# A two-stage attention kernel: the first stage's loop regrouped into slots of two query tiles

## The chip, the cores and the metric

The kernel runs on one core of a Trainium2 chip. The metric is the device time of one execution in microseconds, given as the median of several runs. The profile is one such execution, recorded by the hardware profiler, with all its instructions on the five engines: TensorE (PE, with its weight loads as PEld), VectorE (DVE), ScalarE (ACT), GpSimd (POOL) and the queue SP, which issues DMAs.

## What is computed

The input is x, four sequences of 512 tokens with 128 features, in float32. A causal attention with 16 heads of 64 comes first (stage one), then a network of six layers with local attention and a gated feed-forward part (stage two). Each stage works on a layer-normalised input and is added to what went in. The change touches stage one alone:

```python
q = (x @ Wq).reshape(b, s, HEADS, HEAD_DIM)
k = (x @ Wk).reshape(b, s, HEADS, HEAD_DIM)
v = (x @ Wv).reshape(b, s, HEADS, HEAD_DIM)
scores = SCALE * jnp.einsum('bqhd,bkhd->bhqk', q, k)
causal = jnp.triu(jnp.ones((s, s), dtype=x.dtype), k=1)
scores = scores + MASK_PENALTY * causal
attn = jax.nn.softmax(scores, axis=-1)
out = jnp.einsum('bhqk,bkhd->bqhd', attn, v).reshape(b, s, HEADS * HEAD_DIM)
return out @ Wr
```

The mask is a finite penalty of -50 on keys that lie ahead of the query, so all 512 keys are scored for each query.

## The kernel before

**Tiling.** Stage one goes over 4 sequences b, 8 chunks c of two heads each (128 of the 1024 inner features), and 4 tiles t of 128 queries: 128 `Rows` objects, one for each (b, c, t). All matmuls read float32, but for the penalty, which is bfloat16.

**What one tile does.** `scores` (L210) lays the causal penalty into a tile `ps_sc` of two PSUM banks, one for each head, with a matmul of the identity by `pen` (L216, 512 - 128 t columns per head), and adds q times k in four matmuls (L227; each float32 matmul shows as two passes in the trace, and the two heads lie side by side in the array, 64 rows each). VectorE takes the negative row maximum of both heads (L236). `exponents` (L242) is ScalarE's exponential from PSUM to `pr`, once for each head, with the sum of the row as a second result. `normalise` has the reciprocal of the sums on VectorE (L251) and the product of `pr` with it on GpSimd (L252). `transposes` (L263) brings `pr` to `pT` through two banks `ps_pt`, head 0 copied out by ScalarE (L267), head 1 by VectorE (L269).

**What one chunk does.** `make_q` and `make_k` project the next chunk's q and k (L180, L186); ScalarE scales q out of PSUM (L182), VectorE copies k (L188). `make_v` (L195, copy L202) projects 512 columns of V for one tile of keys; it is called once in nearly each chunk. `times_v1` (L280) multiplies V with `pT` for all 512 queries of a chunk, in two halves of two key tiles, into `ps_o`; it uses the array as two times 64 columns. VectorE copies the result behind the second half (L290). After the eight chunks of a sequence `project_out1` (L295) does the output projection.

**Buffers.** `ps_sc`: 2 tiles (four banks). `ps_pt`: 2 banks. `ps_o`: 1 bank. `ps_pj`: 1 bank, shared by the q, k, V and output projections and by the three steps of each layer normalisation (mean L93, variance L102, scale L110), of which a chunk has at most one. `pr` has 3 buffers, `pT` 2.

**Order.** Each engine works through its instructions in the order in which the program calls them; semaphores order the engines against each other. The loop at L311 takes one tile m per step. A step calls the scores and the maximum of tile m, the exponents and the normalisation of tile m-1, the projection of q (t = 0) or k (t = 1), the transposes of tile m-2, a projection of V (t = 0), half a product with V of the chunk before (t = 2 and 3), and a normalisation step (t = 1).

Of the kernel before, what the change touches and what calls it, by code (L numbers as in the profile page):

```python
# [15 lines left out]
P = 128  # L16
# [4 lines left out]
NC = INNER // P  # L21
# [10 lines left out]
def body(ctx: ExitStack, tc: tile.TileContext, a, out: bass.AP):  # L32
# [5 lines left out]
    nc = tc.nc  # L38
    x = a["x"]
    B, S, _ = x.shape  # L40
    L = a["wqkv"].shape[0]
    NT = S // P
# [9 lines left out]
    mm = nc.tensor.matmul  # L52
# [12 lines left out]
    ident16 = const.tile([P, P], BF16, tag="ident16", name="ident16")  # L65
# [66 lines left out]
    with tc.tile_pool(name="s1", bufs=1) as s1, tc.tile_pool(  # L132
# [6 lines left out]
        pen = s1.tile([P, S], BF16, tag="pen", name="pen")  # L139
# [38 lines left out]
        def make_q(b, c):  # L178
            p = bank1()
            mm(p, lhsT=wq[:, c * P : (c + 1) * P], rhs=xnT[b], start=True, stop=True)  # L180
            q = qs[b, c] = s1.tile([P, S], F32, tag="q1", name="q1", bufs=2)
            nc.scalar.activation(q, p, AF.Copy, scale=0.125)  # L182

        def make_k(b, c):
            p = bank1()
            mm(p, lhsT=wk[:, c * P : (c + 1) * P], rhs=xnT[b], start=True, stop=True)  # L186
            k = ks[b, c] = s1.tile([P, S], F32, tag="k1", name="k1", bufs=2)
            nc.vector.tensor_copy(k, p)  # L188

        def make_v(b, j, t):  # L190

            if t == 0:
                vs[b, j] = s1.tile([P, NT, 512], F32, tag="v1", name="v1", bufs=3)
            p = bank1()
            mm(  # L195
                p,
                lhsT=xnT[b][:, t * P : (t + 1) * P],
                rhs=wv[:, j * 512 : (j + 1) * 512],
                start=True,
                stop=True,  # L200
            )
            nc.vector.tensor_copy(vs[b, j][:, t, :], p)  # L202

        class Rows:
# [5 lines left out]
            def scores(self):  # L210
                b, c, t = self.b, self.c, self.t
                sc = self.sc = ps1.tile([P, 2, S], F32, tag="sc", name="ps_sc", bufs=2)
                for h in range(2):


                    mm(  # L216
                        sc[:, h, t * P : S],
                        lhsT=ident16,
                        rhs=pen[:, 0 : S - t * P],
                        start=True,  # L220
                        stop=False,
                        skip_group_check=True,
                    )
                for k0 in range(0, S, S // 2):
                    for h in range(2):
                        rows = slice(h * HD, (h + 1) * HD)
                        mm(  # L227
                            sc[:, h, k0 : k0 + S // 2],
                            lhsT=qs[b, c][rows, t * P : (t + 1) * P],
                            rhs=ks[b, c][rows, k0 : k0 + S // 2],  # L230
                            start=False,
                            stop=True,
                            skip_group_check=True,
                        )
                self.nm = small.tile([P, 2], F32, tag="nm", name="nm")
                nc.vector.tensor_reduce(self.nm, sc, AX.X, ALU.max, negate=True)  # L236

            def exponents(self):
                self.pr = s1.tile([P, 2, S], F32, tag="pr1", name="pr1", bufs=3)
                self.den = small.tile([P, 2], F32, tag="den", name="den")  # L240
                for h in range(2):
# [5 lines left out]
                        accum_out=self.den[:, h : h + 1],  # L247
                    )

            def normalise(self):  # L250
                nc.vector.reciprocal(self.den, self.den)  # L251
                nc.gpsimd.tensor_tensor(  # L252
                    self.pr, self.pr, self.den.unsqueeze(2).to_broadcast([P, 2, S]), ALU.mult
                )
# [53 lines left out]
        make_q(0, 0)  # L308
        make_k(0, 0)

        for m in range(len(rows) + NT + 1):  # L311
            b, c, t = m // (NC * NT), m // NT % NC, m % NT
            more = b < B
            if more:
                rows[m].scores()
            if 0 < m <= len(rows):
                rows[m - 1].exponents()
                rows[m - 1].normalise()

            bn, cn = (b, c + 1) if c + 1 < NC else (b + 1, 0)  # L320
            if bn < B and t == 0:
                make_q(bn, cn)
            if bn < B and t == 1:
                make_k(bn, cn)
            if 1 < m < len(rows) + 2:
                rows[m - 2].transposes()
            if m < NT:
                make_v(0, 0, m)
            if t == 0 and more:
                if c < NT:  # L330
                    make_v(b, 1, c)
                elif b + 1 < B:
                    make_v(b + 1, 0, c - NT)

            bp, cp = (b, c - 1) if c > 0 else (b - 1, NC - 1)
            if 0 <= bp < B and t >= 2:
                times_v1(bp, cp, t - 2)
            if t == 1 and 1 <= c <= 3 and b + 1 < B:
                if c == 1:
                    norms[b + 1] = norm_x(b + 1)  # L340
                norms[b + 1][c - 1]()
            if b > 0 and c == 1 and t == 0:
                project_out1(b - 1)
                norms1[b - 1] = norm_x1(bank1, b - 1)
            if b in range(1, B) and t == 1 and 4 <= c <= 6:
                norms1[b - 1][c - 4]()


# [519 lines left out]
```

## Time and profile before

| | us |
|---|---|
| median of 3 runs (2391.53 to 2397.76) | 2394.96 |
| profiled execution: its time | 2393.57 |
| profiled execution: its span | 2391.8 |
| stage one, from the first scores to the start of the last L295 | 27.0 to 599.4 |

The mean granted TensorE clock over the span is 0.994. Stage one in stretches, busy time of each engine (the view of windows):

| stretch, us | PE | DVE | ACT | POOL | granted clock |
|---|---|---|---|---|---|
| 100 to 200 | 97.2 | 56.4 | 47.4 | 42.4 | 1.00 |
| 200 to 300 | 97.2 | 63.6 | 48.2 | 43.6 | 1.00 |
| 300 to 400 | 96.9 | 57.3 | 45.8 | 40.2 | 1.00 |
| 400 to 500 | 96.7 | 57.0 | 45.6 | 41.6 | 1.00 |
| 580 to 600 | 16.8 | 8.4 | 8.0 | 9.0 | 1.00 |

A timeline line has the start in us from the start of the span, the duration, the engine, the line, the operation, what it writes and reads, the sizes and how many instructions were merged (x8); brackets give idle time of the engine before it and what ended it. A waits line has who waited for whom, the total in us, how often, and the longest. Ends of matmuls are modelled by the profiler, so the distance from the start of one group to the start of the next is the safer measure of what a group takes.

### The profile page before, as it was taken

Reading aid. Unit: us, or ns where it says so; the run is one execution under the profiler, and the core shown is the slowest. Engines: PE = TensorE matmul, PEld = TensorE weight load, DVE = VectorE, ACT = ScalarE, POOL = GpSimd, SP = SyncE. Lnnn points to the kernel's source line nnn. Section 1 sums busy time; section 2 is a strip of 40 time slices with the busy share of each in tenths; the row PEclk is TensorE's granted clock in tenths of the full one; section 3 lists DMA queues with packets and bytes.
Section 4 is the critical chain, followed back from the end, with each engine's and each line's share of the span. In section 5 each row is a group of like instructions: output and inputs, shape, how many; then the busy total and the mean of one; then the engine's idle time right before and its main releaser. Section 6 shows DMA issues by size and latency. Waiting matters only on the chain.

```text
span 2391.8 us, 81676 instructions
## 1 busy us (share of the span) xinstructions
PE 2252.0 (94%) x35057; PEld 1437.8 (60%) x35088; DVE 1695.7 (71%) x2692; ACT 1305.0 (55%) x2166; POOL 1435.4 (60%) x1897
## 2 busy tenths in 40 slices
PE   7999999999799999999999999999999999999997
PEld 3555555555366666666666666666666666666664
DVE  4655656555677777777877778777877777777774
ACT  3454444444254665655565555566555666555662
POOL 2443444444576677766766766766766767766760
PEclk9999999999999999999999999999999999999998
DMA  3000000000222232222322223223232223322220
GB/s 109 1 1 1 1 1 1 1 1 1 55 64 64 54 92 71 57 70 62 83 70 64 66 61 87 68 57 74 63 91 61 70 57 85 78 55 72 61 58 15
DMA packets 91026, 125.82 MB, mean 53 GB/s; under 512 B 25262, under 2 KB 39468, under 8 KB 90668
## 3 DMA queue, kind: packets, MB, share of 16 engines
q1 hardware_dynamic: 90236, 119.02, 20.3%
q8 instruction: 280, 4.59, 0.9%
q10 hardware_dynamic: 432, 1.57, 0.2%
q14 instruction: 78, 0.64, 0.1%
HBM read 20.41 MB, written 1.05 MB: 9 GB/s over the span
## 4 chain that ended last, share of the span: by engine, by line
PE 79%; DVE 13%; issue 4%; ACT 2%; POOL 2%; DMA 1%; SPq 0%; ACTq 0%; POOLq 0%; DVEq 0%
PE ps_proj L414 19%; PE ps_one L510 10%; PE ps_one L605 7%; PE ps_att L580 6%; PE ps_att L548 6%; PE ps_sc L227 5%; PE ps_o L280 5%; PE ps_pt L263 4%; PE ps_proj L638 3%; PE ps_proj L639 3%; PE ps_proj L652 2%; DVE on L590 2%; POOL pr L252 2%; DVE yt L79 1%; PE ps_pj L180 1%
## 5 line engine op out<-in xcount | busy, mean ns | idle before, releaser
L414 PE MATMUL ps_proj<-wqkv,xs 128*128 128x512 f32 x1152 | 568.3, 616 | 31.1 <-ACT vt L492 22.9
L450 POOL TENSOR_TENSOR rot<-rot,t 128x1024 f32<-128x1024 f32 x192 | 453.0, 2360 | 199.7 <-DVE t L439 197.8
L252 POOL TENSOR_TENSOR pr<-pr,den 128x1024 f32<-128x1024 f32 x128 | 242.2, 1893 | 350.3 <-PE ps_pt L263 188.3
L425 ACT ACTIVATE sq<-ps_proj 128x1024 f32<-128x1024 f32 x192 | 196.7, 1025 | 408.4 <-PE ps_proj L414 358.2
L458 POOL TENSOR_TENSOR rot<-rot,ss 128x1024 f32<-128x1024 f32 x192 | 365.2, 1902 | 15.0
L414 PEld LDWEIGHTS ps_proj<-wqkv,xs 128*128 128x128 f32 x1152 | 198.7, 190 | 218.9 <-issue 155.6
L430 DVE TENSOR_REDUCE ss<-sq 128x16 f32<-128x1024 f32 x192 | 233.2, 1214 | 51.1 <-ACT sq L425 50.4
L236 DVE TENSOR_REDUCE nm<-ps_sc 128x2 f32<-128x1024 f32 x128 | 156.7, 1225 | 129.7 <-PE ps_sc L227 129.7
L435 DVE TENSOR_TENSOR rot<-ps_proj,lt 128x1024 f32<-128x1024 f32 x192 | 233.7, 1217 | 0.0
L439 DVE TENSOR_TENSOR t<-ps_proj,lt 128x1024 f32<-128x1024 f32 x192 | 233.2, 1215 | 0.0
L82 POOL TENSOR_TENSOR yt<-y 128x32 f32<-128x32 f32 x288 | 68.7, 239 | 242.9 <-DVE y L80 227.9
L605 PEld LDWEIGHTS ps_one<-aT,wo 128*128 128x128 f32 x1536 | 186.4, 192 | 45.1 <-issue 44.4
L510 PE MATMUL ps_one<-ident,rot 128*128 128x128 f32 x1536 | 211.0, 280 | 1.2 <-ACT qT L513 0.9
L558 DVE TENSOR_REDUCE mx<-ps_att 128x16 f32<-128x1024 f32 x96 | 117.5, 1224 | 126.2 <-PE ps_att L548 125.0
L605 PE MATMUL ps_one<-aT,wo 128*128 128x128 f32 x1536 | 187.3, 275 | 0.4 <-ACT aT L513 0.4
L242 ACT ACTIVATE pr<-ps_sc,nm 128x512 f32<-128x512 f32 x256 | 174.2, 690 | 20.2 <-DVE den L251 15.6
L589 DVE RECIPROCAL rden<-ps_att 128x8 f32<-128x8 f32 x192 | 39.6, 206 | 195.5 <-PE ps_att L580 186.2
L510 PEld LDWEIGHTS ps_one<-ident,rot 128*128 128x128 f32 x1536 | 165.2, 141 | 20.1 <-issue 1.4
L267 ACT COPY pT<-ps_pt 128x512 f32<-128x512 f32 x128 | 74.7, 584 | 181.8 <-PE ps_pt L263 181.8
L580 PEld LDWEIGHTS ps_att<-vw,pT 64*32 64x32 f32 x9216 | 105.1, 105 | 107.7 <-issue 74.0
L580 PE MATMUL ps_att<-vw,pT 64*32 64x65 f32 x9216 | 129.7, 225 | 36.2 <-DVE on L590 27.7
L263 PEld LDWEIGHTS ps_pt<-ident,pr 128*128 128x128 f32 x1024 | 114.4, 141 | 67.4 <-issue 44.6
(127 smaller groups left out, 4061.3 us busy)
## 6 DMA issues: line engine op xcount, KB each, us to landing
vw<-vt SPq DMA_DIRECT2D x1152, 65.0 KB
vw_first<-vt SPq DMA_DIRECT2D x336, 65.0 KB
wqkv<-in_wqkv_dram SPq DMA_DIRECT2D x18, 512.0 KB
wo<-in_wo_dram SPq DMA_DIRECT2D x6, 512.0 KB
w<-in_w_dram SPq DMA_DIRECT2D x6, 341.0 KB
xr<-in_x_dram SPq DMA_DIRECT2D x4, 256.0 KB
out_dram<-tmp_t SPq DMA_DIRECT2D x4, 256.0 KB
w<-in_w_dram SPq DMA_DIRECT2D x12, 64.0 KB
```

The source lines that it names most:

```text
L252: nc.gpsimd.tensor_tensor(self.pr, self.pr, self.den.unsqueeze(2).to_broadcast([P, 2, S]), ALU.mult)
L263: nc.tensor.transpose(pt[:, k * P : (k + 1) * P], self.pr[:, h, k * P : (k + 1) * P], ident)
L414: mm(p[:, c, :], lhsT=u.xs[:, u.T * P : (u.T + 1) * P], rhs=wpart[j][:, c * 512 : (c + 1) * 512], start=True, stop=True,)
L425: nc.scalar.activation(u.sq, u.p[j], AF.Square)
L430: nc.vector.tensor_reduce(u.ss[:, j * HEADS : (j + 1) * HEADS], heads(u.sq), AX.X, ALU.add)
L435: nc.vector.tensor_tensor(heads(t0), heads(pf), lt[:, u.T, 2 * j].unsqueeze(1).to_broadcast([P, HEADS, HD]), ALU.mult)
L439: nc.vector.tensor_tensor(t1.rearrange("p (h t d) -> p h t d", t=2, d=half), pf.rearrange("p (h t d) -> p h t d", t=2, d=half)[:, :, ::-1, :],
L450: nc.gpsimd.tensor_tensor(u.r[j], u.r[j], u.t1, ALU.add)
L458: nc.gpsimd.tensor_tensor(heads(u.r[j]), heads(u.r[j]), u.ss[:, j * HEADS : (j + 1) * HEADS].unsqueeze(2).to_broadcast([P, HEADS, HD]), AL ...
L510: nc.tensor.transpose(tp[:, c * P : (c + 1) * P], src[:, (4 * g + c) * P : (4 * g + c + 1) * P], ident)
L580: mm(o[j * W : (j + 1) * W, h, c * (HD + 1) : (c + 1) * (HD + 1)], lhsT=u.pT[h * HD : (h + 1) * HD, 4 * g + c, j * W : (j + 1) * W], rhs=u ...
L605: mm(y[:, 0:P], lhsT=wo_w[0][:, c, :], rhs=u.aT[:, c, :], start=(c == 0), stop=(c == NC - 1))
```

## The change

The loop takes two tiles per step, a slot. Slot m has the tiles 2m and 2m+1 ("now") and works off those of slot m-1 ("old"). A chunk is two slots: the even one projects q, the odd one k. On TensorE a slot is half a product with V of an earlier chunk, the scores of both tiles, the penalties of both tiles, the transposes of the first old tile, the projection of q or k, the transposes of the second old tile, and then a projection of V (odd slots) or a normalisation step (even slots).

The first half of a chunk's product with V stands at the head of the odd slot behind the one whose last act is the transposes of the chunk's last tile. The penalty is added behind the scores rather than laid down ahead of them. The maximum, the reciprocal and the product with it become calls of their own (`maximum`, `inverse`, `normalise`); the reciprocals stand behind the second transposes of the slot, the second one also behind V's projection. Buffers, sizes and the number of matmuls stay as they were.

```diff
             def scores(self):
                 b, c, t = self.b, self.c, self.t
                 sc = self.sc = ps1.tile([P, 2, S], F32, tag="sc", name="ps_sc", bufs=2)
-                for h in range(2):
-
-
-                    mm(
-                        sc[:, h, t * P : S],
-                        lhsT=ident16,
-                        rhs=pen[:, 0 : S - t * P],
-                        start=True,
-                        stop=False,
-                        skip_group_check=True,
-                    )
                 for k0 in range(0, S, S // 2):
                     for h in range(2):
                         rows = slice(h * HD, (h + 1) * HD)
...
-                            start=False,
-                            stop=True,
+                            start=(k0 == 0),
+                            stop=False,
                             skip_group_check=True,
                         )
+
+            def penalty(self):
+
+                sc, t = self.sc, self.t
+                for h in range(2):
+                    mm(
+                        sc[:, h, t * P : S],
+                        lhsT=ident16,
+                        rhs=pen[:, 0 : S - t * P],
+                        start=False,
+                        stop=True,
+                        skip_group_check=True,
+                    )
+
+            def maximum(self):
+                sc = self.sc
                 self.nm = small.tile([P, 2], F32, tag="nm", name="nm")
                 nc.vector.tensor_reduce(self.nm, sc, AX.X, ALU.max, negate=True)
...
+            def inverse(self):
+                nc.vector.reciprocal(self.den, self.den)
+
             def normalise(self):
-                nc.vector.reciprocal(self.den, self.den)
                 nc.gpsimd.tensor_tensor(
...
-        for m in range(len(rows) + NT + 1):
-            b, c, t = m // (NC * NT), m // NT % NC, m % NT
-            more = b < B
-            if more:
-                rows[m].scores()
-            if 0 < m <= len(rows):
-                rows[m - 1].exponents()
-                rows[m - 1].normalise()
+        last = len(rows) // 2
+        for m in range(last + 5):
+            b, c, odd = m // (2 * NC), m // 2 % NC, m % 2
+            now = rows[2 * m : 2 * m + 2]
+            old = rows[2 * m - 2 : 2 * m] if m else []
+
+            g = (m - 3) // 2
+            if 0 <= g < B * NC:
+                times_v1(g // NC, g % NC, 1 - odd)
+            for r in now:
+                r.scores()
+            for r in now:
+                r.penalty()
+            if now:
+                now[0].maximum()
+            if old:
+                old[0].transposes()
+            if now:
+                now[0].exponents()
+                now[1].maximum()
 
             bn, cn = (b, c + 1) if c + 1 < NC else (b + 1, 0)
-            if bn < B and t == 0:
-                make_q(bn, cn)
-            if bn < B and t == 1:
-                make_k(bn, cn)
-            if 1 < m < len(rows) + 2:
-                rows[m - 2].transposes()
-            if m < NT:
-                make_v(0, 0, m)
-            if t == 0 and more:
-                if c < NT:
-                    make_v(b, 1, c)
-                elif b + 1 < B:
-                    make_v(b + 1, 0, c - NT)
-
-            bp, cp = (b, c - 1) if c > 0 else (b - 1, NC - 1)
-            if 0 <= bp < B and t >= 2:
-                times_v1(bp, cp, t - 2)
-            if t == 1 and 1 <= c <= 3 and b + 1 < B:
+            if bn < B:
+                (make_k if odd else make_q)(bn, cn)
+            if old:
+                old[1].transposes()
+            if now:
+                now[1].exponents()
+                now[0].inverse()
+                now[0].normalise()
+            if m < 2:
+                make_v(0, 0, 2 * m)
+                make_v(0, 0, 2 * m + 1)
+            if odd and c < NT and b < B:
+                make_v(b, 1, c)
+            elif odd and c >= NT and b + 1 < B:
+                make_v(b + 1, 0, c - NT)
+            if now:
+                now[1].inverse()
+                now[1].normalise()
+            if not odd and 1 <= c <= 3 and b + 1 < B:
                 if c == 1:
                     norms[b + 1] = norm_x(b + 1)
                 norms[b + 1][c - 1]()
-            if b > 0 and c == 1 and t == 0:
+            if b > 0 and c == 1 and odd:
                 project_out1(b - 1)
                 norms1[b - 1] = norm_x1(bank1, b - 1)
-            if b in range(1, B) and t == 1 and 4 <= c <= 6:
+            if b in range(1, B) and not odd and 4 <= c <= 6:
                 norms1[b - 1][c - 4]()
```

## The prediction

> **What bounds the kernel now.** I read the page first, then the waits of stage one (40 to 600 us), then its timeline. Stage one ends with the last output projection, L295, which starts at 599.40 us; nothing behind it changes.
>
> ```profile
> PE 2252.0 (94%) x35057; PEld 1437.8 (60%) x35088; DVE 1695.7 (71%) x2692; ACT 1305.0 (55%) x2166; POOL 1435.4 (60%) x1897
> ```
>
> TensorE is busy 94% of the span. What it waits for in stage one, with total, times and longest:
>
> ```profile
> PE ps_pt L263 <- POOL pr L252: 11.2, 22, 1.3
> PE ps_pj L295 <- DVE v L202: 2.4, 3, 0.8
> PE ps_o L280 <- ACT pT L267: 0.2, 1, 0.2
> ```
>
> So only 13.8 us are waits; the rest is groups of matmuls one behind the other. In the timeline the distance from one start to the next is what a group costs:
>
> ```profile
> 212.62 0.38 PE L216 MATMUL ps_sc<-pen,ident 128*128 128x256 bf16 x2
> 212.93 1.14 PE L227 MATMUL ps_sc<-k,q 64*128 64x256 f32 x8
> 213.99 1.09 PE L263 MATMUL ps_pt<-ident,pr 128*128 128x128 f32 x8
> 215.01 1.94 PE L280 MATMUL ps_o<-pT,v 128*64 128x512 f32 x8
> 216.88 0.28 PE L216 MATMUL ps_sc<-pen,ident 128*128 128x128 bf16 x2
> 217.10 1.13 PE L227 MATMUL ps_sc<-k,q 64*128 64x256 f32 x8
> 219.08 1.09 PE L263 MATMUL ps_pt<-ident,pr 128*128 128x128 f32 x8 [0.85 <-POOL pr L252]
> ```
>
> Scores take 1.07, the product with V 1.87, the penalty 0.21 to 0.53 by its columns, transposes 0.87 (1.02 ahead of the product), a projection 0.94 to 0.96. A chunk of four tiles without a normalisation step is 4.36 + 3.32 + 4.27 + 4.17 = 16.12 us.
>
> Why a group costs more than its columns shows in the single rows of 217.10 to 217.85: the first pair of scores (two heads side by side) holds the array 0.32 us, each later pair 0.215, and 0.093 pass between the end of a group's columns and the next group of another array shape (64 rows, 64 columns, or full). That 0.093 is the same at scores to projection, transposes to product, product to penalty and penalty to scores.
>
> **What the change saves on TensorE.** A chunk changes shape 12 times today (each of four scores in and out, each of two products in and out) and 6 times after (product, both scores, penalties: three per slot). Six changes at 0.093 are 0.56 us; longer first pairs fall from four to two (2 x 0.105), and other groups no longer start behind a change (about 0.1). I take 0.86 a chunk, 27 us over 31 chunks, and the POOL waits of 11.2 go too, since a row's transposes now come a slot later. The step from product to scores, from 64 columns to 64 rows, is in no row; its bounds are 0 and two changes (0.19), and I take one, as all four that are seen are equal. Two scores behind each other have the same shape: 0.215 per pair, with a new first pair (+0.105, 6.5 us over 62 slots) as the upper bound and no lower one, since nothing streams faster in these rows. Penalties behind the scores add as many columns as ahead of them.
>
> **What it adds: two waits per chunk.** I walk a slot from the start of its product, with start-to-start distances from the rows. The built order of instructions shows what each waits for. In both slots scores start at 1.87 and the penalties at 1.87 + 0.32 + 7 x 0.215 + 0.093 = 3.80. The first maximum now needs both tiles' scores and its own two penalties ahead of it; a VectorE consumer starts 0.207 behind the end of a matmul's columns (0.42 behind the start of a last score of 0.213).
>
> ```profile
> 224.74 0.60 ACT L182 ACTIVATE q<-ps_pj 128x512 f32<-128x512 f32 x1 [3.03 <-PE ps_pj L180]
> 225.23 0.58 ACT L267 COPY pT<-ps_pt 128x512 f32<-128x512 f32 x1
> ...
> 34.46 1.23 DVE L236 TENSOR_REDUCE nm<-ps_sc 128x2 f32<-128x1024 f32 x1 [0.71 <-PE ps_sc L227]
> 35.60 0.15 DVE L251 RECIPROCAL den<-den 128x2 f32<-128x2 f32 x1
> 35.67 0.67 DVE L188 COPY k<-ps_pj 128x512 f32<-128x512 f32 x1
> ...
> 36.40 1.13 PE L195 MATMUL ps_pj<-wv,xnT 128*128 128x512 f32 x2 [0.93 <-DVE k L188]
> ```
>
> The columns are start, duration, engine, line and operation, and in brackets the idle time before it. They give the steps from start to start: ACT's q to its copy 0.49; 1.14 from a maximum to the next on VectorE; k's copy 0.67 long, then 0.05 until TensorE starts. The last line shows the very wait that I expect in every odd slot: V's projection wants the only ps_pj bank, which k's copy still reads.
>
> Even slot: the first tile's penalties end at 3.80 + 2 x 0.213; maximum at 4.43, done 5.66; exponents 5.75 (0.09 behind it in most rows) and 2 x 0.66 long; q's scaling at 7.07, pT's copy of the second transposes at 7.57, done 8.15. The product of the next slot reads that copy: it starts at 8.20. TensorE alone would be there at 7.41 (3.80 + 0.75 + 0.87 + 0.96 + 1.02), so 0.79 is wait. Before, two or more groups of the next tile lay between a transpose and its product.
>
> Odd slot: penalties are narrower, maximum at 4.22; VectorE then has, in its queue's order, pT copy 5.36 (1.14 behind a maximum), maximum 5.97 (0.61 behind a copy, the step behind L590 of the same 512 columns in stage two), k copy 7.11, done 7.78; V's projection at 7.83 instead of 6.85. It takes 0.96 and 0.093: the slot is 8.89, 0.98 of it wait. Today V's projection follows q, whose ACT scaling lies under the transposes.
>
> Behind the waiting V projection stand the next product and everything after it on TensorE; behind the k copy wait pT's second copy and the reciprocals, which end early enough: the reciprocals, moved behind the pT, k and V copies on VectorE, start POOL's 1.89 at 8.65 and 10.54, done 10.5 and 12.4; the transposes that read them come at 13.4 and 15.3, so the move costs nothing, and would cost what the 2.9 us of cover were short. The exponents that hold the two score banks end by 9.5 of a slot, the scores that want the second come at 11.1. No DMA is moved. The 18 even slots with a normalisation step also need ps_pj, held by q until 7.72, against 0.22 waited today: 8.78, 8.73 and 8.31 (steps of 0.96, 0.91, 0.49).
>
> **The sum.** Slots 2 to 63. Even: 6 x 8.78 + 6 x 8.73 + 6 x 8.31 + 12 x 8.20 + 7.71 (the last, without q) = 261.0. Odd: 27 x 8.89, three without V at 6.99, the last 6.5, and 3 x 7.9 for L295: 291.2. Slot 2 has no product (-1.87). The first two slots, with V's projections waiting in turn for VectorE as at 29.99 to 37.36 today, put slot 2 at 46.6 (today's tile 4: 43.97). The tail waits for POOL's last two rows: transposes at 9.98 and 11.9 of slot 63, two halves of the product, L295 at 17.3, which is 10.8 behind the slot's end. L295 starts at 46.6 + 550.3 + 10.8 = 607.7, 8.3 later. Against the profiled execution (2393.57, span 2391.8) that is 2401.9; against the median 2394.96 it is 2403.
>
> **A rule against it.** Each slot now has an idle stretch of 0.8 to 1 us. In 580 to 600 us today TensorE idles 1.05, 0.57 and 1.26 us, and the windows view gives a granted clock of 1.00 for that stretch as for all of stage one; I count no loss of clock. The Trainium skill, "TensorE: Matmul & The Clock Gate", section "A second HAM failure mode: psum-queue depth-cycling", says that short idle stretches between groups can make the clock fall to half and back. An estimate from its window of 3.4 us: one such window a chunk would cost 1.7 us, 53 in all, and give 2456. The row decides here.
>
> **Rivals.** (a) Faster: the two waits don't bite, because copies land earlier than my walk says. Without them 13 x 0.79 + 18 x 0.47 + 27 x 0.98 = 45 us go: 2358. For it: ACT is busy 55%. Against: both chains run through queues in fixed order. Chance 0.10. (b) No change: each wait about 0.15 shorter (58 x 0.15 = 9): 2394. The bounds of product-to-scores (62 x 0.09 = 5.8 either way) alone nearly reach it. 0.16. (c) Clearly slower: VectorE doesn't start the next operation 0.09 before the one ahead of it has ended, as behind its maxima today, but 0.03 behind, as where one small operation feeds the next (L83 behind L82). That is 0.12 at three places of the odd slot and one of the even, 27 x 0.36 + 31 x 0.12 = 13 more: 2416. It decides once the odd slot passes 9.2. Against it: in stage two VectorE starts 0.09 early behind L430 and L439 too. 0.14. The built order shows the moves as the diff says them, so that the change does nothing is no case.
>
> **Numbers.** My forecast, both waits in full, has 0.60; its own range, from product-to-scores either way, is 2397 to 2409. About 0.3% (7.2 us) can be told from no change, and the forecast is 8.3: of its 0.60 I put 0.20 within. Faster 0.10; same 0.16 + 0.20 = 0.36; slower 0.40 + 0.14 = 0.54. The range takes in (b) and the lower part of (c): 2389 to 2418.
>
> **What would show it.** In stage one after: L263's waits for POOL gone; TensorE waiting some 0.8 us at the product for ACT's pT copy and 1.0 at V's projection for k's copy; product to scores 1.87; slots near 8.2 and 8.9; L295 near 608. Wrong if these waits are below half, if product to scores is far from 1.87, or if the clock falls.

## The result, and the profile after

The changed kernel takes 2416.9 us (median of 5 runs, 2408.12 to 2419.03) where the kernel before takes 2396.45 (5 runs on the same chip): a ratio of 1.008, 95% interval 1.0055 to 1.0106. The forecast was 8.3 us more; the medians are 20.4 apart, the two profiled spans 23.0 (2414.8 and 2391.8).

The last output projection (L302 after, L295 before) starts at 623.46 us, where it started at 599.40 and the forecast had 607.7. Stage one is 24.1 longer and the rest of the span 1.1 shorter, so all of it lies in stage one. After the change the tile's lines are: scores L216, penalty L229, maximum L241, exponents L247, reciprocal L256, GpSimd's product L259, transposes L270 with copies L274 (ScalarE) and L276 (VectorE), product with V L287, its copy aT L297. First the engines' line of the page after:

```profile
PE 2230.5 (92%) x35056; PEld 1446.4 (60%) x35088; DVE 1697.1 (70%) x2692; ACT 1300.6 (54%) x2166; POOL 1435.9 (59%) x1897
```

TensorE has 21.5 us less work on its record and the span is 23.0 longer: 44.5 us more idle. The view of waits, stage one after (40 to 600 us; who waited for whom, total, times, longest), names it:

```profile
PE ps_pj L195 <- DVE k L188: 26.4, 28, 1.1
PE ps_o L287 <- ACT pT L274: 10.7, 12, 0.9
PE ps_pt L270 <- DVE pT L276: 6.2, 6, 1.0
...
PE ps_pj L110 <- ACT q L182: 2.5, 6, 0.4
```

The first two lines are the forecast's two waits, 0.9 each. The third, six times 1.0, was not forecast. The timeline of TensorE after, an odd slot from one product to the next, and the head of the even slot behind it:

```profile
126.45 1.94 PE L287 MATMUL ps_o<-pT,v 128*64 128x512 f32 x8 [0.89 <-ACT pT L274]
128.32 2.00 PE L216 MATMUL ps_sc<-k,q 64*128 64x256 f32 x16
130.25 0.50 PE L229 MATMUL ps_sc<-pen,ident 128*128 128x256 bf16 x4
130.59 1.05 PE L270 MATMUL ps_pt<-ident,pr 128*128 128x128 f32 x8
131.47 1.02 PE L186 MATMUL ps_pj<-xnT,wk 128*128 128x512 f32 x2
132.33 1.04 PE L270 MATMUL ps_pt<-ident,pr 128*128 128x128 f32 x8
134.28 1.13 PE L195 MATMUL ps_pj<-wv,xnT 128*128 128x512 f32 x2 [0.91 <-DVE k L188]
135.34 1.94 PE L287 MATMUL ps_o<-pT,v 128*64 128x512 f32 x8
137.21 2.00 PE L216 MATMUL ps_sc<-k,q 64*128 64x256 f32 x16
```

Product to scores is 128.32 - 126.45 = 1.87, the value taken. The odd slot is 135.34 - 126.45 = 8.89; its wait of 0.89 at the head is the one that the forecast counts at the end of the even slot. From scores to scores, even slots without a normalisation step take 8.22 throughout; those with a mean, variance or scale step take 8.80, 8.73 and 8.33. The walk had 8.20, 8.78, 8.73 and 8.31. So the normal slots are right to 0.02 us, and a chunk takes 17.11 where it took 16.12.

What the walk did not have starts in the slots with a variance step. The timeline after, VectorE, GpSimd and TensorE together, from such a slot (20) into the odd one behind it (21):

```profile
220.59 3.74 POOL L259 TENSOR_TENSOR pr<-pr,den 128x1024 f32<-128x1024 f32 x2 [12.75 <-DVE den L256]
222.16 0.35 DVE L79 TENSOR_SCALAR yt<-rs 128x4 int32<-128x4 int32 x1
222.54 1.82 DVE L80 TENSOR_SCALAR y<-yt 128x4 int32<-128x4 int32 x1
...
226.66 1.22 DVE L241 TENSOR_REDUCE nm<-ps_sc 128x2 f32<-128x1024 f32 x1
...
228.53 0.66 PE L270 MATMUL ps_pt<-ident,pr 128*128 128x128 f32 x4 [1.04 <-DVE pT L276]
230.26 1.19 PE L195 MATMUL ps_pj<-wv,xnT 128*128 128x512 f32 x2 [1.07 <-DVE k L188]
231.38 3.52 PE L287 MATMUL ps_o<-pT,v 128*64 128x512 f32 x8
```

And the same two small operations in the kernel before:

```profile
211.23 1.89 POOL L252 TENSOR_TENSOR pr<-pr,den 128x1024 f32<-128x1024 f32 x1 [2.37 <-PE ps_pt L263]
...
212.99 0.17 DVE L79 TENSOR_SCALAR yt<-rs 128x4 int32<-128x4 int32 x1
213.19 0.17 DVE L80 TENSOR_SCALAR y<-yt 128x4 int32<-128x4 int32 x1
```

L80, on four columns, takes 0.17 before and 1.82 after (1816 to 1820 ns in all six slots). After, GpSimd's two products run one behind the other from 220.59 to 224.33; the middle of that is 222.46. L79 ends at 222.51 and L80 at 224.36, each just behind the end of one product. Before, the product ended at 213.12, and the small operations ran behind it at 0.17. So VectorE stood while GpSimd worked. The late start of the maximum (226.66) makes the transposes wait 1.04, and V's projection 1.07 where 0.91 is usual: odd slots behind a variance step take 10.30, not 8.89.

The last line shows a second loss: the product of slot 21 takes 3.52 where its like took 1.94. The windows view after has it too (the stretch, its length, then busy time and instructions of TensorE, its weight loads, VectorE, ScalarE and GpSimd, then TensorE's granted clock, and two columns on DMA):

```profile
224.00:228.00 4.00, 3.49 (x28) 2.33 (x24) 3.59 (x15) 0.61 (x2) 0.33 (x1) 1.00 0.00 0
228.00:232.00 4.00, 2.40 (x8) 1.01 (x10) 3.39 (x6) 3.25 (x9) 0.96 (x1) 0.90 0.02 4
232.00:236.00 4.00, 4.00 (x18) 1.54 (x16) 0.94 (x3) 0.00 (x0) 2.79 (x2) 0.67 0.00 0
...
616.00:620.00 4.00, 3.24 (x12) 2.10 (x13) 1.38 (x2) 0.81 (x2) 0.74 (x1) 0.61 0.00 0
```

Stage one after has two such stretches, this one and one at 286 us. Both stand directly behind the waits of 1.04 and 1.07 in an odd slot that follows a variance step; slots 21 and 27 take 11.95 and 11.91. The other odd slots behind a variance step have such a wait too and no such stretch. The last window is a third stretch, in the tail of stage one.

### The profile page after: what moved, and what is told of

The parts are those of the page before. It is cut to its first block, busy times and chain, and to the rows that moved or that the text cites. A ratio compares the mean times of both kernels' runs of the same rounds, so it can differ in the third digit from the quotient of the medians.

```text
span 2414.8 us, 81635 instructions
## 1 busy us (share of the span) xinstructions
PE 2230.5 (92%) x35056; PEld 1446.4 (60%) x35088; DVE 1697.1 (70%) x2692; ACT 1300.6 (54%) x2166; POOL 1435.9 (59%) x1897
## 4 chain that ended last, share of the span: by engine, by line
PE 58%; DVE 11%; issue 3%; ACT 2%; POOL 0%; ACTq 0%; POOLq 0%
PE ps_proj L436 19%; PE ps_one L532 10%; PE ps_one L627 7%; PE ps_att L602 6%; PE ps_att L570 5%; PE ps_proj L660 2%; PE ps_proj L661 2%; PE ps_proj L674 2%; DVE on L612 2%; DVE yt L79 1%; DVE rot L457 1%; DVE t L461 1%; ACT vt L514 1%; PE ps_att L559 1%; PE ps_one L93 1%
## 5 line engine op out<-in xcount | busy, mean ns | idle before, releaser
L259 POOL TENSOR_TENSOR pr<-pr,den 128x1024 f32<-128x1024 f32 x128 | 239.9, 1894 | 375.5 <-DVE den L256 375.5
L241 DVE TENSOR_REDUCE nm<-ps_sc 128x2 f32<-128x1024 f32 x128 | 156.0, 1219 | 124.4 <-PE ps_sc L229 124.4
L274 ACT COPY pT<-ps_pt 128x512 f32<-128x512 f32 x128 | 75.1, 587 | 300.6 <-PE ps_pt L270 300.6
L627 PEld LDWEIGHTS ps_one<-aT,wo 128*128 128x128 f32 x1536 | 186.3, 192 | 45.3 <-issue 44.5
L247 ACT ACTIVATE pr<-ps_sc,nm 128x512 f32<-128x512 f32 x256 | 175.2, 696 | 23.1 <-DVE nm L241 23.0
L532 PEld LDWEIGHTS ps_one<-ident,rot 128*128 128x128 f32 x1536 | 165.8, 142 | 20.4 <-issue 2.8
L514 ACT COPY vt<-ps_proj 128x512 f32<-128x512 f32 x192 | 103.1, 589 | 85.6 <-PE ps_proj L436 84.6
```

Source lines behind the costliest of these rows:

```text
L247: nc.scalar.activation(self.pr[:, h, :], self.sc[:, h, :], AF.Exp, bias=self.nm[:, h : h + 1], accum_out=self.den[:, h : h + 1],)
L259: nc.gpsimd.tensor_tensor(self.pr, self.pr, self.den.unsqueeze(2).to_broadcast([P, 2, S]), ALU.mult)
L532: nc.tensor.transpose(tp[:, c * P : (c + 1) * P], src[:, (4 * g + c) * P : (4 * g + c + 1) * P], ident)
L627: mm(y[:, 0:P], lhsT=wo_w[0][:, c, :], rhs=u.aT[:, c, :], start=(c == 0), stop=(c == NC - 1))
```

## The experiments

All edits are made to the changed kernel, unless said otherwise. The runs came in three groups, each on one chip and with its own runs of the kernel before (medians 2393.08, 2392.91 and 2393.36), so the ratios are what to compare. The table gives the usual slot lengths of each profile, from scores to scores, and the granted clock from 60 to 600 us. "Even" and "odd" are slots without a normalisation step in or ahead of them; e8_penalty_ahead is measured from product to product.

| run | median, us | ratio to before (95%) | even | odd | odd behind variance | clock |
|---|---|---|---|---|---|---|
| after | 2416.9 | 1.008 (1.0055–1.0106) | 8.22 | 8.89 | 10.30–11.95 | 0.99 |
| e1_newton_pool | 2404.17 | 1.0042 (1.0026–1.0059) | 8.22 | 8.89 | 8.89 | 1.00 |
| e1b_norm_on_vector | 2409.91 (one run) | – | 8.22 | 8.89 | 9.75 | 0.99 |
| e2_k_copy_first | 2382.54 | 0.996 (0.9945–0.9976) | 8.22 | 7.88 | 9.17 | 1.00 |
| e3_exp_behind_copy | 2426.02 | 1.0124 (1.0108–1.014) | 8.11 | 8.89 | 13.6–14.7 | 0.97 |
| e5_product_behind | 2447.91 | 1.0232 (1.0216–1.0248) | 8.19 | 10.34 | 10.2–10.6 | 0.99 |
| e6_maxima_first | 2478.51 | 1.0358 (1.0344–1.0371) | 9.47 | 8.03 | 10.1–10.3 | 0.95 |
| e7_all | 2473.95 | 1.0345 (1.0316–1.0375) | 9.47 | 8.03 | 9.5–10.9 | 0.94 |
| e8_penalty_ahead | 2432.42 | 1.0175 (1.0158–1.0193) | 8.60 | 9.20 | 10.4 | 1.00 |
| e9_copy_behind | 2402.45 | 1.0039 (1.0025–1.0054) | 7.42 | 8.03 | 10.95–12.67 | 0.98 |
| e10_copy_behind_all | 2370.54 | 0.9911 (0.9892–0.993) | 7.42 | 8.03 | 8.03 | 1.00 |
| e11_k_copy_and_newton | 2374.58 | 0.9931 (0.9913–0.9949) | 8.22 | 7.88 | 7.88 | 1.00 |

**The variance's small operations on GpSimd.** A queue of their own takes them out from under the products:

```diff
-        nc.vector.tensor_scalar(ti, v.bitcast(I32), 1, None, ALU.logical_shift_right)
-        nc.vector.tensor_scalar(y.bitcast(I32), ti, -1.0, 1597463007.0, ALU.mult, ALU.add)
+        if pool_seed:
+            nc.gpsimd.tensor_scalar(y.bitcast(I32), v.bitcast(I32), -0.5, 1597463007.0, ALU.mult, ALU.add)
+        else:
+            nc.vector.tensor_scalar(ti, v.bitcast(I32), 1, None, ALU.logical_shift_right)
+            nc.vector.tensor_scalar(y.bitcast(I32), ti, -1.0, 1597463007.0, ALU.mult, ALU.add)
...
-            rsqrt(rs, NT, nc.vector)
+            rsqrt(rs, NT, eng, pool_seed=eng is nc.gpsimd)
```

`eng` is GpSimd for the six variance steps inside the loop, and VectorE otherwise.

> The changed kernel, with the 13 small operations of stage one's six variance steps on GpSimd behind its two products, not on VectorE beside them (the starting value in one operation). In the changed kernel's trace L80 takes 1.82 us there instead of 0.17, ends with GpSimd's second product, and the odd slot behind is 10.3 us instead of 8.89; two half-clock stretches in stage one follow such slots. Theory (the two engines exclude each other): the odd slots behind a variance step fall to 8.9, no half-clock stretch is left inside stage one, the time falls by 8 to 12 us against the changed kernel. Rival (those slots are long for another reason, such as the PSUM bank held by q): they stay near 10.3 and the time stays within 3 us.

The timeline of GpSimd in this run; its lines stand three further down (L262 is L259):

```profile
223.69 3.74 POOL L262 TENSOR_TENSOR pr<-pr,den 128x1024 f32<-128x1024 f32 x2 [14.45 <-DVE den L259]
227.51 0.19 POOL L80 TENSOR_SCALAR y<-rs 128x4 int32<-128x4 int32 x1
227.79 0.20 POOL L85 TENSOR_TENSOR yt<-y 128x4 f32<-128x4 f32 x1
```

They now follow the products in GpSimd's own queue, 0.28 us each, and nothing on VectorE waits. The odd slots behind a variance step are 8.89 like all others. By the ratios the kernel is 0.4% faster than after, some 9 us, which the theory asked for. A miss: stretches at half clock did not vanish. The profile has one at the start and one at about 207 us, where the slot with the output projection took 18.50 instead of 16.81; e1b_norm_on_vector, the next run, has two more such slots. Behind a variance step neither run has one.

**The same place from the other side: GpSimd's products of these slots on VectorE.** This gives VectorE 2 x 1.23 us more work in the slots in question, and takes away what excludes it.

```diff
+            eng = nc.vector if var_step else nc.gpsimd
...
-                now[0].normalise()
+                now[0].normalise(eng)
...
-                now[1].normalise()
+                now[1].normalise(eng)
```

> The changed kernel, with the two products of exponents and reciprocals of each variance slot on VectorE instead of GpSimd, so that VectorE has some 2.4 us more to do there and GpSimd nothing. If the engines exclude each other, L80 is 0.17 us again and the odd slot behind is shorter than 10.3, about 9.6 (VectorE then reaches the next maximum some 0.7 us late), in spite of the added work. If VectorE is simply overloaded there, the slot becomes longer, about 12.

VectorE's timeline in this run:

```profile
221.74 1.23 DVE L259 TENSOR_TENSOR pr<-pr,den 128x1024 f32<-128x1024 f32 x1
222.89 0.15 DVE L104 TENSOR_SCALAR rs<-ps_pj 128x4 f32<-128x4 f32 x1
223.08 0.17 DVE L79 TENSOR_SCALAR yt<-rs 128x4 int32<-128x4 int32 x1
223.28 0.17 DVE L80 TENSOR_SCALAR y<-yt 128x4 int32<-128x4 int32 x1
```

L80 is back at 0.17 and the slot at 9.75, shorter than 10.30 although VectorE has more to do. A VectorE that is merely overloaded would have made the slot longer. The exclusion is shown from both sides. The Trainium skill, "SBUF — State Buffer", section "Who interferes with whom", says that VectorE and GpSimd share a pair of ports, that `tensor_scalar` can take it in its fast mode, and that whoever comes second is blocked for the whole instruction; L80's 1.82 us beside a GpSimd product of 1.89 agrees. No run here shows which port it was.

**k's copy ahead of the second maximum** in odd slots, so that V's projection gets its bank earlier:

```diff
-                now[1].maximum()
+                if not odd:
+                    now[1].maximum()
...
                 (make_k if odd else make_q)(bn, cn)
+            if now and odd:
+                now[1].maximum()
```

> The changed kernel, with k's copy ahead of the second tile's maximum on VectorE in odd slots; TensorE's order is untouched. Theory (V's projection waits only for that copy): the copy starts at about 6.15 of the slot and ends at 6.83, the wait of 0.95 us falls to below 0.1, ordinary odd slots are 7.95 instead of 8.89, the time falls by 24 to 28 us. Rival (VectorE's queue is the bound of the slot, and the wait moves to the second maximum, the exponents and the next slot's scores): odd slots and even slots together stay within 0.3 us of 17.1, the time falls by less than 8 us.

The timeline of VectorE, and behind it the waits of TensorE (40 to 600 us), in this run:

```profile
126.71 0.68 DVE L276 COPY pT<-ps_pt 128x512 f32<-128x512 f32 x1
127.42 0.69 DVE L188 COPY k<-ps_pj 128x512 f32<-128x512 f32 x1
128.03 1.22 DVE L241 TENSOR_REDUCE nm<-ps_sc 128x2 f32<-128x1024 f32 x1
```

```profile
PE ps_o L287 <- ACT pT L274: 11.6, 14, 0.9
PE ps_pt L270 <- DVE pT L276: 6.2, 6, 1.0
```

The 26.4 us behind k's copy are gone; the other two waits stay. The 19 ordinary odd slots fell by 1.01, the slots behind a variance step by 1.13 where no half-clock stretch stood, and the three with the output projection by 0.53; this profile has no half-clock stretch between 60 and 600 us. The last slot starts 30.5 us earlier. By the ratios the time falls by 1.2%, some 29 us, where 24 to 28 were expected; the medians, from different groups of runs, are 34 apart. Moving one VectorE call makes the kernel faster than before.

**ScalarE's pT copy ahead of the first exponents** in even slots:

```diff
-                now[0].exponents()
+                if odd:
+                    now[0].exponents()
...
+                if not odd:
+                    now[0].exponents()
                 now[1].exponents()
```

> The changed kernel, with the first tile's exponents in even slots behind q's scaling and pT's copy on ScalarE instead of ahead of them; nothing else moves. Theory (the product with V waits only for ScalarE's copy): ordinary even slots fall from 8.22 to 7.4 us, those with a normalisation step by 0.4, the time falls by 15 to 20 us. Rival (the exponents, now 1.7 us later, hold the score bank or GpSimd's product, and the wait moves to the next slot's scores or transposes): even slots near 7.4, but odd slots longer by as much, the time falls by less than 6 us.

The timeline of TensorE in this run:

```profile
127.78 2.42 PE L287 MATMUL ps_o<-pT,v 128*64 128x512 f32 x8 [0.29 <-ACT pT L274]
130.14 2.00 PE L216 MATMUL ps_sc<-k,q 64*128 64x256 f32 x16
```

The product's wait shrinks from 0.89 to 0.29, but the scores behind it start 2.36 later instead of 1.87: an even slot is 8.11, 0.11 less. The product reads two copies of pT, head 0 from ScalarE and head 1 from VectorE. In this run ScalarE's ends at 127.73 and the product starts at 127.78; VectorE's ends at 128.22 and the first matmul of head 1 starts at 128.26, where in after it started with head 0's (both at 126.45). In after, VectorE's copy ended at 126.29 and ScalarE's at 126.40, so that taking ScalarE out of the way could give no more than 0.11. The theory fell. Its rival, that the score bank or GpSimd's product holds up the next slot, isn't what happened either, since ordinary odd slots stay at 8.89. The odd slots behind a variance step grew by 3.3 to 4.4 us; the transposes wait there up to 2.7 for VectorE's copy, and why it comes so late stays open.

**The product behind both penalties**, nothing else moved:

```diff
-            g = (m - 3) // 2
-            if 0 <= g < B * NC:
-                times_v1(g // NC, g % NC, 1 - odd)
             for r in now:
                 r.scores()
             for r in now:
                 r.penalty()
+            g = (m - 3) // 2
+            if 0 <= g < B * NC:
+                times_v1(g // NC, g % NC, 1 - odd)
```

> The changed kernel with one part undone: the product with V stands behind both tiles' penalties instead of in front of both tiles' scores. Theory (the product in front is what waits for ScalarE's copy of pT, and moving it back only uncovers the next wait): the product waits no more, even slots are near 7.4 us, but the second tile's scores now come 1.9 us earlier in the slot and wait some 1.2 us for the exponents that hold the score bank, so even and odd slot together stay at 17.1 to 17.6 and the time within 10 us of the changed kernel. Rival (the product's place alone is the fault): even slots 7.4, odd slots 8.9, the time falls by 15 us or more.

The waits of TensorE in this run:

```profile
PE ps_pj L195 <- DVE k L188: 22.2, 28, 1.1
PE ps_sc L216 <- ACT pr L247: 17.6, 24, 1.2
PE ps_pt L270 <- DVE pT L276: 6.3, 28, 0.8
```

The product no longer waits for a pT copy; the scores wait for the exponents of the tile before, and odd slots grew to 10.34, while even ones stay at 8.19 where 7.4 was expected. The time is 1.5% above after, more than the theory allowed.

**Both maxima and the exponents first as well:** product behind the penalties, then both maxima, the first exponents, the first transposes and the second exponents.

```diff
                 now[0].maximum()
+                now[1].maximum()
+                now[0].exponents()
             if old:
                 old[0].transposes()
             if now:
-                now[0].exponents()
-                now[1].maximum()
+                now[1].exponents()
...
             if now:
-                now[1].exponents()
                 now[0].inverse()
```

> The product behind both tiles' penalties, and VectorE's and ScalarE's order to suit: both maxima first, the first tile's exponents ahead of the pT copies, the second tile's between the copy and q's scaling. Theory (the waits come from the order on the two queues, not from TensorE's work): even slots without a normalisation step near 7.4 us, odd slots near 8.0, 15.4 for a chunk against 16.1 for today's loop; VectorE and GpSimd still meet in the six variance steps, worse than now (2 us each). The time is 25 to 35 us below the changed kernel and below the kernel before. Rival (two-tile slots are bound by these queues whatever their order): a chunk stays above 16.5 us.

The odd slot became 8.03, as expected; the even one 9.47 instead of 7.4. The timeline of this run says why:

```profile
134.61 1.94 PE L287 MATMUL ps_o<-pT,v 128*64 128x512 f32 x8
...
136.60 0.69 DVE L297 COPY aT<-ps_o 128x512 f32<-128x512 f32 x1 [3.90 <-PE ps_o L287]
137.20 2.35 DVE L241 TENSOR_REDUCE nm<-ps_sc 128x2 f32<-128x1024 f32 x2
...
140.29 1.06 PE L270 MATMUL ps_pt<-ident,pr 128*128 128x128 f32 x8 [1.86 <-DVE pT L276]
```

The copy of the finished product (aT) is called inside the product's function, so it stands ahead of both maxima in VectorE's queue. VectorE idles 3.90 us on it; in the last two of these the scores and penalties of both tiles are there (the last penalty starts at 134.36). My walk had left that copy out.

**The same with the variance's operations on GpSimd and one projection of V in each of the first four slots** (two in each of the first two before):

```diff
-            if m < 2:
-                make_v(0, 0, 2 * m)
-                make_v(0, 0, 2 * m + 1)
+            if m < NT:
+                make_v(0, 0, m)
```

> As the run with both maxima first, and in addition the small operations of the variance steps on GpSimd behind its products, and one projection of V in each of the first four slots instead of two in each of the first two. Expected another 10 to 18 us less: odd slots behind a variance step like all others, the third slot starting 2 to 4 us earlier. About 2367 us, 1.2% below the kernel before. If the variance steps are not what lengthens those slots, it gains less than 5 us over the other run.

It has the same even slot, 9.47, and the lowest clock of all, 0.94. By the ratios it gains some 3 us over the run before, not 10 to 18, and the two intervals overlap. By its own sign that would speak against the variance step as the cause of the long slots; but the long slots of this run hold half-clock stretches (the scores of slot 21, at 244.36, take 3.78 instead of 2.00), so it decides nothing, and the runs e1 and e10 do.

**The penalty ahead of each tile's scores again,** two-tile slots kept:

```diff
             for r in now:
-                r.scores()
-            for r in now:
                 r.penalty()
+                r.scores()
```

Start and stop flags are exchanged with it.

> The changed kernel with one part undone: each tile's penalty ahead of its own scores, as before, with the slots of two tiles kept. By the shape changes TensorE has some 0.4 us more per slot (five changes instead of three, a second long first pair), but the first maximum comes 0.8 us earlier. Theory (the slot ends with the queues, not with TensorE): even slots fall to about 7.8 us, odd ones are 8.9 to 9.3, the time stays within 8 us of the changed kernel. Rival (the shape changes saved are what counts, slots are bound by TensorE): both slots grow by 0.4, the time rises by 20 us or more.

Slots grew by 0.38 and 0.31 us, and the time by about 0.95% against after (1.0175 to 1.008), more than the theory allowed and as much as its rival asked for. That part of the change does save: with the penalties ahead, a slot of two tiles changes array shape three times more (3 x 0.093) and has a second long first pair of scores (0.105), 0.38 by the prediction's figures.

**The cause of 9.47, tested.** The aT copy is split from the product and called behind both maxima and the first exponents; the rest is as in e6_maxima_first.

```diff
-            if half == 1:
-                at = aTs[b, c] = s1.tile([P, S], F32, tag="aT1", name="aT1", bufs=NC + 2)
-                nc.vector.tensor_copy(at, o)
+        def copy_v1(b, c):
+            at = aTs[b, c] = s1.tile([P, S], F32, tag="aT1", name="aT1", bufs=NC + 2)
+            nc.vector.tensor_copy(at, os_[b, c])
...
                 now[0].exponents()
+            if 0 <= g < B * NC and not odd:
+                copy_v1(g // NC, g % NC)
```

> The order with both maxima first, with one thing changed: VectorE's copy of the finished product with V (aT) is called behind both maxima and the first tile's exponents, not ahead of them. Theory: that run's even slot took 9.47 us only because the copy, which waits for the product, stood ahead of both maxima in VectorE's queue. Then the even slot without a normalisation step falls from 9.47 to 7.3-7.6, the odd one stays at 8.0-8.1, the transposes wait for VectorE's pT copy in hardly any slot, and the time falls from 2478 by 50 to 100 us, to 2375-2430: 1.9 x 31 = 59 us from the even slots alone, more if the half-clock stretches go with the waits. The slots with a variance step stay about 2 us longer than their neighbours. Rival: what makes the even slot long is the product itself, which now stands behind the penalties, so that the old tiles' transposes and the copies behind them all start 1.9 us later; the even slot then stays above 9.0 and the time above 2460.

> The same, with the variance's small operations on GpSimd in stage one and one projection of V in each of the first four slots instead of two in each of the first two. Theory: slots as in the run above (7.3-7.6 and 8.0-8.1), those with a variance step within 0.4 us of those with a mean, and the first slots some 5 us shorter: 12 to 22 us below the run above, 2360-2400. Rival: if the half-clock stretches come from the order itself (as in the two runs with both maxima first: 13 and 17 of them) and not from the long waits, both runs have ten or more of them and stay above 2400.

Even slots fell from 9.47 to 7.42, the time by 76 us. What is left in e9_copy_behind is the exclusion, larger here; its timeline:

```profile
218.47 1.26 DVE L79 TENSOR_SCALAR yt<-rs 128x4 int32<-128x4 int32 x1
219.76 1.82 DVE L80 TENSOR_SCALAR y<-yt 128x4 int32<-128x4 int32 x1
...
227.27 1.27 PE L270 MATMUL ps_pt<-ident,pr 128*128 128x128 f32 x8 [2.92 <-ACT pT L274]
228.33 1.92 PE L195 MATMUL ps_pj<-wv,xnT 128*128 128x512 f32 x2
```

Now both small operations stand, the transposes wait 2.92, and V's projection behind them takes 1.92 where 1.13 is usual: half clock again. With the variance's operations on GpSimd (e10_copy_behind_all) the slot behind is 8.03, no slot behind the fourth is out of its pattern, and the time is 2370.54. The step from the one to the other is 32 us by the medians and 25.4 by the profiled spans, more than the 12 to 22 expected. By the slots of the two profiles, 2.9 to 4.6 us come from each of the six slots behind a variance step (22.2 together) and 0.5 to 1.2 from the slots behind four of these (3.3): where a slot is longer than the wait of 2.9 explains, the clock had fallen. Spreading V's projections gave only 0.9, the start of slot 4 at 70.20 instead of 71.12.

**k's copy first and the variance on GpSimd, together:**

> The changed kernel with two edits together: k's copy ahead of the second maximum in odd slots, and the variance's small operations on GpSimd. Theory: they mend two different places, so they add: odd slots 7.9, those behind a variance step the same instead of 9.17, so 6 x 1.2 = 7 us below the run with k's copy alone: 2372-2379, a ratio of 0.991 to 0.994 to the kernel before. Rival: with k's copy first, the six odd slots behind a variance step wait for something else as well (GpSimd has 13 more small operations in them), and the time stays within 3 us of the run with k's copy alone, 2380-2386.

The two gains add: 8.0 us below k's copy alone by the medians, 7 by the ratios, and odd slots of 7.88, those behind a variance step included. The rival, that these slots wait for something else too, is refuted.

## Why the prediction was right in direction and short in size

**The saving on TensorE and its condition.** The order of TensorE's groups does save. Without its waits the chunk after is 17.11 - 0.91 - 0.89 = 15.31 us against 16.12 before, 0.81, where the forecast said 0.86. GpSimd's 11.2 us of waits went; 2.1 are left in the tail.

**The two waits.** Right in place, engine and size. The walk gave 0.79 and 0.98; the profile's idle times are 0.89 and 0.91, the slots fit to 0.02. What the walk didn't show is that VectorE's copy of pT ends only 0.11 before ScalarE's, so that the wait at the product has two causes of nearly the same length. Undoing only one of them (k's copy first) turned the ratio from 1.008 to 0.996, so these waits, and not the two-tile slots, are what makes the change lose. Rival (a) was refuted by the waits view, rival (b) by the slot lengths. Rival (c) held that VectorE would start 0.03 behind the end of the operation ahead, so that the odd slot passes 9.2; it is 8.89, so (c) is refuted although its time, 2416, is nearly the measured one. The forecast's own range, 2397 to 2409, was missed; that the measured 2416.9 lies inside the wide one, 2389 to 2418, is luck, since its upper part was meant for (c).

**What was mis-sized.** Start of L302: 623.46 against 607.7, 15.8 us. Four terms of the sum:

- "three without V at 6.99" and "27 x 8.89" for odd slots. Six of these follow a variance step: five are 1.41 above, the sixth 8.10 against 6.99, together 8.2. The step that failed is the variance step, which I costed at its TensorE side (8.73, right) and not at VectorE's. The sentence "the reciprocals ... start POOL's 1.89 at 8.65 and 10.54 ... the move costs nothing" looked at who waits for GpSimd, not at whom GpSimd keeps from working. The move put both products beside the variance's small operations. Shown by e1_newton_pool and e1b_norm_on_vector.
- "I count no loss of clock ... The row decides here." Two stretches in stage one, 3.06 - 1.41 = 1.65 and 1.61: 3.3 us. The row I relied on was no proof: there the idle stretches of 0.57 and 1.26 us lie 1.1 us apart and the clock stays at 1.00; in after, the waits of 1.04 and 1.07 lie 0.7 apart and it falls. What the Trainium skill, "TensorE: Matmul & The Clock Gate", section "A second HAM failure mode: psum-queue depth-cycling", says, that short idle stretches between groups can make the clock fall, was right in kind; the estimate of one window a chunk was far too much: 2 in 31 chunks.
- "put slot 2 at 46.6": it is 49.05. The first scores (27.21) take 3.79 and their penalties 1.27 instead of 2.00 and 0.70, which is 2.36 of the 2.45 us; from the start of these scores to the next projection 5.19 pass, and 2.69 in slot 2. k's projection just ahead takes 2.07 both before (2.08) and after, so TensorE starts slow in both, and stays slow 5 us longer after. The windows view reads 1.00 there in both profiles, but the trace's records of the clock begin only at 27.22 before and at 33.22 after, where the rows get fast.
- the tail, "10.8 behind the slot's end": L302 starts 18.85 behind the start of slot 63, not 17.3. There the last transposes take 1.92 instead of 1.09, and the last two halves of the product 4.89 where they took 4.19 before: 1.5 of the 1.55. The clock in that window is 0.61.

Together 8.2 + 3.3 + 2.45 + 1.55 = 15.5 of the 15.8. By cause: about half is VectorE standing behind GpSimd, about half TensorE running at a lower rate.

**What stays open.** Which idle makes the clock fall. e2 and e11 keep the product's waits of 0.9 and run at 1.00; e6 and e7, with 1.9 in every even slot, run at 0.95 and 0.94; in e9 the same wait of 2.9 is followed by a half-clock stretch in four of six places.

The traces give a part of the answer. In each of them all changes of the granted clock lie a whole number of 3.413 us apart, so stage one can be cut into stretches of that length. In after, TensorE is busy 1.60, 1.34 and 1.31 us in the stretches just ahead of the half-clock ones at 231.19, 285.81 and 616.90 us. No other stretch from 33.22 us to the start of L302 has under 1.74. The waits of slots 21 and 27 lie nearly whole in one such stretch; those behind the other variance steps are cut by a border, and where the borders fall differs from profile to profile. In the row of before that the forecast relied on, the lowest is 1.69 (590.42 to 593.83), and the clock held. This is no full rule: in e5, half-clock stretches follow some with TensorE busy 2.4 to 2.5 us while some with 1.85 have none behind them.

At the start, the two profiles with the penalty ahead of the scores, before and e8, reach full clock at 27.2 and 27.8 us, the eleven with the scores first at 30.0 to 33.3. With the penalty ahead, it runs while the scores wait for k's copy (26.05 in before, where after waits 0.78). No run tests either of the two by itself.

**The versions that beat both kernels** are e2_k_copy_first, e11_k_copy_and_newton and e10_copy_behind_all. The last has the lowest time, 0.9911 (0.9892 to 0.993) of the time before; its interval overlaps that of e11. It keeps two-tile slots and penalties behind the scores. The product stands behind the penalties, so that it covers the maxima. Its chunk is 7.42 + 8.03 = 15.45.

## What to carry to other kernels

When calls are regrouped, walk one period of every engine's queue by start-to-start distances; then walk each exceptional period too, and list which VectorE and GpSimd operations now lie side by side. A wait that appears on the bounding engine is often one call standing ahead of another in an engine that is half idle: here the order of two VectorE operations was worth some 29 us, and the place of a copy inside a helper 2 us in each even slot. Ask of each wait what would end it next: where two copies end 0.11 apart, speeding up one gains no more than that. And price a new wait above its own length, because TensorE's clock may fall behind it.

## What the hardware showed

- A 4-column `tensor_scalar` on VectorE took 1.82 us instead of 0.17 while GpSimd ran a product (six of six). Maxima, copies from PSUM and reciprocals ran beside GpSimd's products at their usual lengths: the V copy at 231.49 took 0.69.
- GpSimd does the small operations in 0.28 us each from start to start, VectorE in 0.20.
- One stretch at half clock (0.50 for 3.41 us) made a slot 1.6 us longer; such stretches came behind waits of TensorE, but not behind each. In every profile they begin a whole number of 3.413 us apart. At the start TensorE ran at half rate while the windows view said 1.00, as the trace had no record of the clock there yet.
- Slots repeat to 0.01 us over hundreds of microseconds, so that one slot out of its pattern shows a loss at once.
